# Edge values from the row's diagonal element, with a VectorE comparison of the whole matrix, in a two-layer graph kernel

## The chip, the cores and the metric

The kernel runs on one core of one Trainium2 chip. The metric is the device time of one execution in microseconds (us). Before the change the median of three runs is 389.42 us (389.2 to 390.23).

## The reference

2708 nodes have 128 features each, and a 2708 x 2708 matrix `adj` holds the weighted edges. In the inputs a row's nonzero elements are all equal (a 0/1 mask, with the diagonal always set, divided by the row's count). Layer 0 works on the hyperbolic ball:

```python
XW = mobius_matvec(W, X)
gamma = 2.0 / jnp.maximum(1.0 - jnp.sum(XW * XW, -1, keepdims=True), EPS)
nominator = A_hat @ (gamma * XW)
denominator = _clamp_abs(A_hat @ (gamma - 1.0))
...
x = _layernorm(x + _L0_gnn_ref(x, adj, L0_gnn_W), axis=-1)
```

Layer 1 passes a message over every edge, and the GELU stands inside the sum:

```python
s = x @ msg_w[:, :D].T
d = x @ msg_w[:, D:].T
messages = gelu(s[:, None, :] + d[None, :, :] + msg_b)
aggregated = einsum('ijd,ij->id', messages, adj)
h = gelu(concat([x, aggregated]) @ upd_w.T + upd_b) + x
x = _layernorm(x + layernorm(h) * ln_w + ln_b)
```

(Left out of layer 0: the Mobius scalings by 0.5 and by the row sum, log, relu and exp.) An edge that is zero contributes nothing, so only the nonzero elements of `adj` need a GELU. The kernel finds them on the chip.

## The kernel before

The 2708 rows are padded to 22 blocks of 128. The host sends `adj` transposed and tiled (`adj_t`, diagonal set to zero) and the diagonal apart, as columns of `pack` (`dg`).

**Layer 0**, `layer0(b)`, takes one block of rows. SyncE (SP) loads the transposed slab `aT` (128 x 2816 f32, 1408 KB, L317; two buffers). ScalarE (ACT) turns it into signs, `sgn`, and counts them (L319, 2.55 us, one buffer). TensorE (PE) multiplies the slab with the features `y`: 22 matmuls in fp32 (L324), which the generator interrupts at the tiles in `BREAKS` so that other work can be issued between them. VectorE (DVE) adds the diagonal's part (L328) and a few sums (L334).

**Edge lists.** `keys` multiplies the signs with bf16 keys, so that each target row holds numbers that encode the sources of its edges (L350), and DVE takes the largest eight of each segment (L358). `extract` turns them into lists of edges, in two stages. The first counts edges, makes prefix sums on PE (L397, L398) and builds `R`, a 128 x 128 matrix per list tile that says which row each of the 128 edges belongs to (L409 on ACT, L412 and L414 on DVE). The second multiplies `R` with the codes (L438), and gets for each edge its row number `rid` (L444) and its source `J` (L447). There are 25 lists in 99 list tiles of 128 edges. L448 then computes `F`, the flat position of the edge in `adj`, and for each of the 99 list tiles GpSimd (POOL) starts an indirect DMA that fetches 128 single elements into a column of `V` (L191, called from `extract`).

The order of the work is partly written out by hand: the loop at L543 to L569 steps the generators of three consecutive blocks alternately. The framework's scheduler then fixes each engine's queue, which runs in order.

`layer0_end` finishes blocks 0 to 15 as soon as they are there and blocks 16 to 21 at the end (`CHUNKS`). It is a long chain of small DVE operations with some ACT and PE, and it writes `d` of the reference to a table in HBM (L535, on SP's queue, which also issues the slabs). After it come the messages of nodes to themselves: `gd`, a GELU (L583) and one multiplication with the diagonal element per block (L585, 22 on ACT).

**Layer 1.** `messages` works through a block's list tiles, up to four at a time (a quad, 29 in all). POOL gathers the sources' rows of the table into `dd` (L191, 99 again, 512 bytes per edge). PE spreads `s` over the edges with `R` (L652). DVE adds (L657), ACT applies the GELU (L658). DVE builds `rv`, a matrix that has the edge's value at the edge's row (L654, one per list tile). PE multiplies `dd` with `rv` and accumulates a block in `ag` (L660). `own` adds the node's own message (L669). ACT copies `ag` out of PSUM (L691 and L702, 30 in all), and `update` and `finish` apply the last matmuls, GELU and normalizations. The buffers `dd` are a ring of seven quads (`RING`); the early tiles of blocks 2 to 7 are gathered into a slab buffer of layer 0. Tiles whose sources lie in blocks 0 to 15 (`soon`) may be gathered once the first half of the table is written. POOL's queue is in order too, so gathers into `V` and into `dd` stand in one line.

At the end a few counters are compared (`flags`, `cnt`), and a dense branch computes the result again if a list did not hold all edges. It isn't entered with these inputs.

The lines that matter:

```python
        F = small.tile([P, TMAX], U32, name="F", bufs=3)
...
            nc.vector.scalar_tensor_tensor(
                F[:, k0:k1], J[:, t], float(b * P * N - 1), rid[:, t], op0=OP.add, op1=OP.add
            )
        for t in range(t0, t0 + n):
            gather(V[:, t : t + 1], adj.rearrange("i (j o) -> (i j) o", o=1), F[:, t - t0 : t - t0 + 1])
...
                nc.vector.tensor_scalar(
                    rv[:, k, :], iotaN, rid[:, t : t + 1], V[:, t : t + 1], op0=OP.is_equal, op1=OP.mult
                )
```

Of the kernel before, what the change touches and what calls it, by code (L numbers as in the profile page):

```python
# [10 lines left out]
F32 = mybir.dt.float32  # L11
U32 = mybir.dt.uint32
# [3 lines left out]
OP = mybir.AluOpType  # L16
# [59 lines left out]
def hyperbolic_then_message_kernel(  # L76
# [4 lines left out]
    x_nm: bass.AP,  # L81
    x_t: bass.AP,
    pack: bass.AP,
    table: bass.AP,
    out: bass.AP,
):
# [79 lines left out]

    R = big.tile([P, NT, P], F32, name="R")
    J = const.tile([P, NT], U32, name="J")
    V = const.tile([P, NT], F32, name="V")
    rid = const.tile([P, NT], F32, name="rid")  # L170
    top = const.tile([P, NC], F32, name="top")
    limit = const.tile([P, NT], F32, name="limit")
# [5 lines left out]
    nc.gpsimd.memset(deg, 0.0)  # L178
    oe = const.tile([P, NL, 2], F32, name="oe")
    signs = const.tile([P, NB], F32, name="signs")  # L180
    poss = const.tile([P, NL], F32, name="poss")
    cap = const.tile([P, NL], F32, name="cap")
    least = const.tile([P, NL], F32, name="least")
# [6 lines left out]
    def gather(o, src, at):  # L190
        nc.gpsimd.indirect_dma_start(  # L191
            out=o, out_offset=None, in_=src, in_offset=bass.IndirectOffsetOnAxis(ap=at, axis=0)
        )
# [5 lines left out]
    def bank(name, bufs=2):  # L199
        return ps.tile([P, 512], F32, name=name, bufs=bufs)  # L200
# [10 lines left out]

    def cols(n):
        count[0] += 1
        return sc.tile([P, n], F32, name=f"c{count[0]}")

    def rsqrt(v, n, pool=None):

# [91 lines left out]
            y[:, g : g + n, :D], mx[:, g : g + n, :], c[:, g : g + n].unsqueeze(2).to_broadcast([P, n, D])  # L309
        )  # L310

    ss, ssp = cols(NB), cols(NB)

    def layer0(b):

        aT = stream.tile([P, NB, P], F32, name="aT")
        nc.sync.dma_start(aT, adj_t[b])  # L317
        sgn = stream.tile([P, NB, P], BF16, name="sgn", bufs=1)
        nc.scalar.activation(sgn, aT, AF.Sign, accum_out=signs[:, b : b + 1])  # L319
        op = bank("mp")  # L320
        for j in range(NB):
            if j in BREAKS:
                yield
            nc.tensor.matmul(  # L324
                op[:, : D + 2], lhsT=aT[:, j, :], rhs=y[:, j, :], start=(j == 0), stop=(j == NB - 1)
            )

        nc.vector.scalar_tensor_tensor(  # L328
            nom[:, b, :], y[:, b, :], dg[:, b : b + 1], op[:, : D + 2], op0=OP.mult, op1=OP.add
        )  # L330
        v, t = nom[:, b, :D], small.tile([P, D], F32, name="junk")
        nc.scalar.activation(t, v, AF.Square, accum_out=ss[:, b : b + 1])
        t = small.tile([P, D], F32, name="junk_p", bufs=1)
        nc.vector.scalar_tensor_tensor(  # L334
            t, v, 0.0, v, op0=OP.max, op1=OP.mult, accum_out=ssp[:, b : b + 1]
        )
        yield sgn
# [28 lines left out]
    def extract(l):  # L366
# [2 lines left out]
        C = wa + wb  # L369

        def tmp(name, dt=F32, w=CMAX):
            return small.tile([P, w], dt, name=name)[:, :C]

        tk = top[:, c0 : c0 + C]
        u0, u1 = 8 * (wa > 0), C - 8 * (wb > 0)
# [51 lines left out]
            )  # L427
        z = zs[l % 2][:, : C + 1]
        nc.vector.scalar_tensor_tensor(z[:, 1:], scan, SPAN, code, op0=OP.mult, op1=OP.add)
        F = small.tile([P, TMAX], U32, name="F", bufs=3)  # L430
        step = 512 // (C + 1)
        for k0 in range(0, n, step):
            k1 = min(n, k0 + step)
            w = k1 - k0
            t = slice(t0 + k0, t0 + k1)
            sp = bank("sel", 1)[:, : w * (C + 1)].rearrange("p (t c) -> p t c", t=w)
            for k in range(w):
                nc.tensor.matmul(sp[:, k, :], lhsT=R[:, t0 + k0 + k, :], rhs=z, start=True, stop=True)  # L438

            dist = small.tile([P, 512], F32, name="work", bufs=3)[:, : w * C].rearrange("p (t c) -> p t c", t=w)  # L440
            nc.vector.tensor_tensor(  # L441
                dist, sp[:, :, 1:], place[:, k0:k1].unsqueeze(2).to_broadcast([P, w, C]), op=OP.subtract
            )
            nc.scalar.copy(rid[:, t], sp[:, :, 0])  # L444
            near = small.tile([P, TMAX], F32, name="near")[:, :w]
            nc.vector.tensor_reduce(near, dist, axis=AX.X, op=OP.min, apply_absolute_value=True)
            nc.vector.scalar_tensor_tensor(J[:, t], near, -1.0, limit[:, t], op0=OP.add, op1=OP.min)  # L447
            nc.vector.scalar_tensor_tensor(  # L448
                F[:, k0:k1], J[:, t], float(b * P * N - 1), rid[:, t], op0=OP.add, op1=OP.add
            )  # L450
        for t in range(t0, t0 + n):
            gather(V[:, t : t + 1], adj.rearrange("i (j o) -> (i j) o", o=1), F[:, t - t0 : t - t0 + 1])

    x1, x1T = x_sb, xT
    s_nm = mx
# [1 line left out]
    def layer0_end(b0, b1):  # L457

        n = b1 - b0
        sb = slice(b0, b1)  # L460

        den, r = nom[:, sb, D], nom[:, sb, D + 1]
        di, t, v, e, f = (cols(n) for _ in range(5))
# [112 lines left out]

    gd = nom
    for ins in last.values():  # L580
        ctx.enter_context(tc.issue_after(ins.ins))
    for g, n in quads:
        nc.scalar.activation(gd[:, g : g + n, :D], gd[:, g : g + n, :D], AF.Gelu)  # L583
        for k in range(n):
            nc.scalar.mul(gd[:, g + k, :D], gd[:, g + k, :D], dg[:, g + k : g + k + 1])  # L585
    xlb = y
    for g, n in quads:
        nc.vector.tensor_add(xlb[:, g : g + n, :D], x1[:, g : g + n, :], wide(rowvec["lb"], n))
# [53 lines left out]
    def messages(b, ag, tiles, first, final, bins, room=ring):  # L642

        for q, k0 in enumerate(range(0, len(tiles), 4)):
            ts = tiles[k0 : k0 + 4]
            w = len(ts)
            dd = room(w)
            X = bank(bins[q % len(bins)]).rearrange("p (t d) -> p t d", d=D)[:, :w, :]
            rv = edge.tile([P, 4, P], F32, name="rv", bufs=3)
            for k, t in enumerate(ts):  # L650
                gather(dd[:, k, :], table[: SPLIT * P] if t in soon else table, J[:, t : t + 1])
                nc.tensor.matmul(X[:, k, :], lhsT=R[:, t, :], rhs=s_nm[:, b, :], start=True, stop=True)  # L652

                nc.vector.tensor_scalar(  # L654
                    rv[:, k, :], iotaN, rid[:, t : t + 1], V[:, t : t + 1], op0=OP.is_equal, op1=OP.mult
                )
            nc.vector.tensor_tensor(dd, X, dd, op=OP.add)  # L657
            nc.scalar.activation(dd, dd, AF.Gelu)  # L658
            for k in range(w):
                nc.tensor.matmul(  # L660
                    ag[:, :P],
                    lhsT=dd[:, k, :],
                    rhs=rv[:, k, :],
                    start=(first and k0 == 0 and k == 0),
                    stop=(final and k0 + k == len(tiles) - 1),
                )

    def own(b, ag):
        nc.tensor.matmul(ag[:, :P], lhsT=gd[:, b, :D], rhs=ident, start=True, stop=False)  # L669
# [17 lines left out]
    for b in range(EARLY):  # L687
        ag = bank("ag", 1)
        own(b, ag)
        messages(b, ag, early[b], False, True, ["X"], roomy)  # L690
        nc.scalar.copy(gd[:, b, :D], ag[:, :P])  # L691
    for g0, gn in GROUPS:
        h = gd[:, g0 : g0 + gn, :D]
        for b in range(g0, g0 + gn):
            ag = bank("mp")
            agT = edge.tile([P, P], F32, name="agT")
            if b < EARLY:
                messages(b, ag, late[b], True, True, ["X", "kx"])
            else:
                own(b, ag)  # L700
                messages(b, ag, early[b] + late[b], False, True, ["X", "kx"])
            nc.scalar.copy(agT, ag[:, :P])  # L702
            update(h, b - g0, b, [agT, gd[:, b, :D]] if b < EARLY else [agT])
        finish(h, g0, gn, fin, last=(g0 + gn == NB))

# [36 lines left out]
        flags[:, 1:2], flags[:, 1:2], float(P * sum(len(v[1]) for v in LISTS)), None, op0=OP.not_equal  # L742
    )

    cnt = sc.tile([P, 2], F32, name="cnt")
    nc.vector.tensor_reduce(cnt[:, 0:1], signs, axis=AX.X, op=OP.add)
    nc.vector.tensor_reduce(cnt[:, 1:2], deg.rearrange("p l k -> p (l k)"), axis=AX.X, op=OP.add)
    bp = bank("sel", 1)
    nc.tensor.matmul(bp[:, 0:2], lhsT=ones, rhs=flags, start=True, stop=True)
    nc.tensor.matmul(bp[:, 2:4], lhsT=ones, rhs=cnt, start=True, stop=True)  # L750
    tot = sc.tile([P, 4], F32, name="tot")
    nc.scalar.copy(tot, bp[:, 0:4])
    nc.vector.tensor_tensor(tot[:, 2:3], tot[:, 2:3], tot[:, 3:4], op=OP.not_equal)
    nc.vector.tensor_add(tot[:, 0:1], tot[:, 0:1], tot[:, 1:2])
    nc.vector.tensor_add(tot[:, 0:1], tot[:, 0:1], tot[:, 2:3])
    flag = sc.tile([P, 1], I32, name="flag")
    nc.vector.tensor_copy(flag, tot[:, 0:1])

    dense = nc.values_load(flag[0:1, 0:1], min_val=0, max_val=2 * P + 1)
    with tc.If(dense > 0):  # L760
        with tc.tile_pool(name="dn", bufs=1) as dn:
            room = R.rearrange("p t i -> p (t i)")
# [32 lines left out]
]  # L795


def by_partition(a, w):

    n = a.shape[0]  # L800
    nb = (n + P - 1) // P
    whole = np.zeros((nb * P, w), a.dtype)
    whole[:n] = a.reshape(n, w)
    return whole.reshape(nb, P, w).transpose(1, 0, 2).reshape(P, nb * w)


def layouts(x, adj, w0, msg_w, msg_b, upd_w, upd_b, ln_w, ln_b):
# [8 lines left out]
    xt[:, :n] = x.T  # L816
    parts = [w0] + [w[:, h * P : (h + 1) * P].T for w in (msg_w, upd_w) for h in (0, 1)]
    parts += [np.broadcast_to(v, (P, P)) for v in (upd_b, ln_w, ln_b, msg_b)]
    parts += [msg_b.reshape(P, 1), by_partition(np.diagonal(adj), 1)]
    return {  # L820
        "adj_t": np.ascontiguousarray(t),
        "x_nm": by_partition(x, P),
        "x_t": xt,
        "pack": np.ascontiguousarray(np.concatenate(parts, axis=1)),
    }


# [31 lines left out]
```

## Time and profile before

| | us |
|---|---|
| median of the runs | 389.42 |
| the profiled execution | 504.16 |
| its span, first to last instruction | 502.5 |
| PE busy | 333.5 |
| DVE busy | 275.9 |
| ACT busy | 208.0 |
| POOL busy | 203.5 |

A profile is one execution under the profiler. Here that execution is 114.7 us longer than the median run, so a length in the profile isn't a length in a run, while the duration of one instruction can be used. Busy time is the time in which an engine worked on an instruction; "mean ns" is the duration of one. A releaser is the instruction for which an engine waited. The stages in the profile: 0 to 26.5 us setup, to 293.7 us layer 0 (one L328 per block, at 38.2, 45.2, 57.0, 71.4, 85.2, 99.2, 119.8, 133.0, then every 7.7 to 8.7 us until 198.1, the last at 293.65), to 335 us the end of layer 0 for the last blocks, then layer 1. The last table gather starts at 451.75, the last matmul of `messages` ends near 473.

### The profile page before, as it was taken

Reading aid. Unit: us, or ns where it says so; the run is one execution under the profiler, and the core shown is the slowest. Engines: PE = TensorE matmul, PEld = TensorE weight load, DVE = VectorE, ACT = ScalarE, POOL = GpSimd, SP = SyncE. Lnnn points to the kernel's source line nnn. Section 1 sums busy time; section 2 is a strip of 40 time slices with the busy share of each in tenths; the row PEclk is TensorE's granted clock in tenths of the full one; section 3 lists DMA queues with packets and bytes.
Section 4 is the critical chain, followed back from the end, with each engine's and each line's share of the span. In section 5 each row is a group of like instructions: output and inputs, shape, how many; then the busy total and the mean of one; then the engine's idle time right before and its main releaser. Section 6 shows DMA issues by size and latency. Waiting matters only on the chain.

```text
span 502.5 us, 7784 instructions
## 1 busy us (share of the span) xinstructions
PE 333.5 (66%) x2427; PEld 297.2 (59%) x2427; DVE 275.9 (55%) x1474; ACT 208.0 (41%) x562; POOL 203.5 (40%) x297
## 2 busy tenths in 40 slices
PE   4269788674899989797973111538397697679620
PEld 4269677564889878795862001338395576557410
DVE  2979546433666565798740067248272226376671
ACT  2827325432657465794650022135032112326521
POOL 5301454571644525222257707722616572470000
PEclk9759779885999999998995555657679557798855
DMA  8306322223345544433421101110201120111100
GB/s 341 167 2 232 115 84 79 88 98 116 118 132 214 193 156 164 184 117 115 137 80 37 52 7 31 52 53 15 49 12 37 42 54 17 38 42 48 32 23 20
DMA packets 16237, 45.14 MB, mean 90 GB/s; under 512 B 5626, under 2 KB 11150, under 8 KB 13374
## 3 DMA queue, kind: packets, MB, share of 16 engines
q1 hardware_dynamic: 9710, 37.43, 20.6%
q0 software_dynamic: 6336, 6.55, 5.4%
q10 hardware_dynamic: 144, 0.60, 0.4%
q8 instruction: 20, 0.33, 0.3%
q14 instruction: 27, 0.22, 0.1%
HBM read 41.74 MB, written 2.83 MB: 89 GB/s over the span
## 4 chain that ended last, share of the span: by engine, by line
PE 32%; DVE 21%; issue 16%; another core or an unknown queue 14%; ACT 10%; DMA 4%; POOL 1%; DVEq 0%; POOLq 0%; ACTq 0%; SPq 0%
PE mp L324 7%; PE X L652 4%; PE mp L660 4%; PE kx L350 4%; PE sel L438 3%; DVE top L358 2%; ACT nom L635 2%; ACT sgn L319 2%; PE ag L660 2%; PE sel L612 1%; PE sel L613 1%; PE sel L610 1%; DMA xT<-in_x_t_dram 1%; DMA V<-in_adj_dram,F 1%
## 5 line engine op out<-in xcount | busy, mean ns | idle before, releaser
L191 POOL DMA_INDIRECT V<-in_adj_dram,F x99 | 94.9, 959 | 156.2 <-DVE top L358 31.0
L324 PE MATMUL mp<-y,aT 128*128 128x130 f32 x968 | 129.2, 288 | 1.4 <-DVE y L308 0.9
L324 PEld LDWEIGHTS mp<-y,aT 128*128 128x128 f32 x968 | 120.1, 199 | 2.3 <-DVE y L308 1.1
L191 POOL DMA_INDIRECT dd<-table_dram,J x81 | 78.1, 965 | 83.7 <-ACT agT L702 21.7
L319 ACT ACTIVATE sgn<-aT 128x2816 bf16<-128x2816 f32 x22 | 56.1, 2548 | 24.5 <-issue 20.5
L350 PE MATMUL kx<-kd,sgn 128*128 128x128 bf16 x484 | 41.5, 240 | 26.6 <-issue 19.1
L350 PEld LDWEIGHTS <-sgn 128*128 128x128 bf16 x484 | 33.3, 108 | 40.1 <-issue 31.4
L652 PE MATMUL X<-mx,R 128*128 128x128 f32 x198 | 41.1, 357 | 16.9 <-DVE dd L657 6.9
L654 DVE TENSOR_SCALAR rv<-iotaN,rid,V 128x128 f32<-128x128 f32 x99 | 30.1, 351 | 32.6 <-remote 20.0
L652 PEld LDWEIGHTS X<-mx,R 128*128 128x128 f32 x198 | 36.2, 265 | 19.2 <-DVE dd L657 7.5
L438 PE MATMUL sel<-z,R 128*128 128x49 f32 (+4 forms) x198 | 31.4, 299 | 23.3 <-DVE R L414 9.6
L438 PEld LDWEIGHTS sel<-z,R 128*128 128x128 f32 x198 | 28.3, 213 | 25.8 <-DVE R L414 10.4
L358 DVE MAX8 top<-kx 128x8 f32<-128x128 f32 (+3 forms) x152 | 28.6, 236 | 19.9 <-remote 14.8
L441 DVE TENSOR_TENSOR work<-sel,place 128x144 f32<-128x144 f32 (+11 forms) x29 | 11.7, 403 | 40.5 <-remote 30.9
L409 ACT ACTIVATE work<-iota,mid 128x512 f32<-128x512 f32 (+3 forms) x53 | 26.8, 553 | 5.5 <-DVE mid L402 5.4
L657 DVE TENSOR_TENSOR dd<-X,dd 128x384 f32<-128x384 f32 (+3 forms) x29 | 15.2, 526 | 21.7 <-remote 7.5
L444 ACT COPY rid<-sel 128x3 f32<-128x3 f32 (+5 forms) x29 | 4.7, 162 | 46.0 <-DVE work L441 36.3
L660 PE MATMUL mp<-rv,dd 128*128 128x128 f32 x116 | 21.6, 321 | 3.1 <-ACT dd L658 3.1
L402 DVE SCALAR_TENSOR_TENSOR mid<-sel,deg 128x2 f32<-128x2 f32 x25 | 3.9, 155 | 35.7 <-ACT oe L399 35.7
L610 PE MATMUL sel<-pk,xT 128*128 128x128 f32 x44 | 12.6, 377 | 16.4 <-ACT nom L614 10.4
L658 ACT ACTIVATE dd<-dd 128x384 f32<-128x384 f32 (+3 forms) x29 | 13.7, 497 | 20.3 <-DVE dd L657 14.5
L399 ACT COPY oe<-sel 128x2 f32<-128x2 f32 x25 | 4.0, 159 | 43.2 <-PE kx L350 25.9
(204 smaller groups left out, 614.6 us busy)
## 6 DMA issues: line engine op xcount, KB each, us to landing
aT<-in_adj_t_dram SPq DMA_DIRECT2D x22, 1408.0 KB, 6.7
V<-in_adj_dram,F POOLq DMA_INDIRECT x99
xT<-in_x_t_dram SPq DMA_DIRECT2D x2, 704.0 KB
x_sb<-in_x_nm_dram SPq DMA_DIRECT2D x2, 704.0 KB
out_dram<-nom SPq DMA_DIRECT2D x21, 64.0 KB, 1.6
dd<-table_dram,J POOLq DMA_INDIRECT x81
table_dram<-dt SPq DMA_DIRECT2D x5, 256.0 KB
pk<-in_pack_dram ACTq DMA_DIRECT2D x1, 587.5 KB
```

The lines of the kernel that those rows point to most:

```text
L191: nc.gpsimd.indirect_dma_start(out=o, out_offset=None, in_=src, in_offset=bass.IndirectOffsetOnAxis(ap=at, axis=0))
L319: nc.scalar.activation(sgn, aT, AF.Sign, accum_out=signs[:, b : b + 1])
L324: nc.tensor.matmul(op[:, : D + 2], lhsT=aT[:, j, :], rhs=y[:, j, :], start=(j == 0), stop=(j == NB - 1))
L350: nc.tensor.matmul(kp[:, i * P : (i + 1) * P], lhsT=sgn[:, j, :], rhs=kd[:, q, :], start=False, stop=(i == len(groups) - 1 and j == j1 - 1),)
L358: nc.vector.max(top[:, c : c + 8], seg[:, s, :])
L409: nc.scalar.activation(r0, iota[:, k0 * P : k1 * P], AF.Abs, scale=2.0, bias=mid[:, k : k + 1])
L438: nc.tensor.matmul(sp[:, k, :], lhsT=R[:, t0 + k0 + k, :], rhs=z, start=True, stop=True)
L610: nc.tensor.matmul(up[:, :D], lhsT=x1T[:, s], rhs=wT[:, 2, :], start=True, stop=False)
L652: nc.tensor.matmul(X[:, k, :], lhsT=R[:, t, :], rhs=s_nm[:, b, :], start=True, stop=True)
L654: nc.vector.tensor_scalar(rv[:, k, :], iotaN, rid[:, t : t + 1], V[:, t : t + 1], op0=OP.is_equal, op1=OP.mult)
L657: nc.vector.tensor_tensor(dd, X, dd, op=OP.add)
L660: nc.tensor.matmul(ag[:, :P], lhsT=dd[:, k, :], rhs=rv[:, k, :], start=(first and k0 == 0 and k == 0), stop=(final and k0 + k == len(tiles ...
```

## The change

All of a row's edges take the row's diagonal element as their value. That makes the values unnecessary inside the sum: `rv` becomes 0/1, the own message is no longer multiplied, and the sum `ag` is multiplied with the diagonal once per block (`scaled`), while it is copied out of PSUM. A new input `diag` holds the diagonal as one row; it is loaded broadcast over the partitions, once per block in layer 0 (`vb`, on SP's queue) and once per copy in layer 1 (`v`, on ACT's queue). The gathers of `V` and the positions `F` go. In layer 0, DVE compares every element of the slab with the diagonal element of its row and counts the equal ones; at the end the count must be the number of edges, and the diagonal must be positive, or the dense branch is taken. Some small buffers become single, and the columns of `cols` are reused between the stages.

```diff
@@ def cols
-        return sc.tile([P, n], F32, name=f"c{count[0]}")
+        return sc.tile([P, NB], F32, name=f"c{count[0]}")[:, :n]
...
@@ def layer0
+        vb = stream.tile([P, P], F32, name="vb")
+        nc.sync.dma_start(vb, diag[:, b * P : (b + 1) * P].to_broadcast([P, P]))
         aT = stream.tile([P, NB, P], F32, name="aT")
         nc.sync.dma_start(aT, adj_t[b])
         sgn = stream.tile([P, NB, P], BF16, name="sgn", bufs=1)
         nc.scalar.activation(sgn, aT, AF.Sign, accum_out=signs[:, b : b + 1])
+
+        eq = stream.tile([P, NB, P], mybir.dt.uint8, name="eq", bufs=1)
+        nc.vector.scalar_tensor_tensor(
+            eq, aT, 1.0, vb.unsqueeze(1).to_broadcast([P, NB, P]),
+            op0=OP.mult, op1=OP.is_equal, accum_out=same[:, b : b + 1],
+        )
...
@@ def extract
-            return small.tile([P, w], dt, name=name)[:, :C]
+            return small.tile([P, w], dt, name=name, bufs=2 if name in ("m", "whole") else 1)[:, :C]
...
-        F = small.tile([P, TMAX], U32, name="F", bufs=3)
...
-            nc.vector.scalar_tensor_tensor(
-                F[:, k0:k1], J[:, t], float(b * P * N - 1), rid[:, t], op0=OP.add, op1=OP.add
-            )
-        for t in range(t0, t0 + n):
-            gather(V[:, t : t + 1], adj.rearrange("i (j o) -> (i j) o", o=1), F[:, t - t0 : t - t0 + 1])
...
@@ own messages
         nc.scalar.activation(gd[:, g : g + n, :D], gd[:, g : g + n, :D], AF.Gelu)
-        for k in range(n):
-            nc.scalar.mul(gd[:, g + k, :D], gd[:, g + k, :D], dg[:, g + k : g + k + 1])
...
@@ def messages
-                nc.vector.tensor_scalar(
-                    rv[:, k, :], iotaN, rid[:, t : t + 1], V[:, t : t + 1], op0=OP.is_equal, op1=OP.mult
+            k = 0
+            while k < w:
+                n = next((i for i in range(1, w - k) if ts[k + i] != ts[k] + i), w - k)
+                nc.vector.tensor_tensor(
+                    rv[:, k : k + n, :],
+                    iotaN.unsqueeze(1).to_broadcast([P, n, P]),
+                    rid[:, ts[k] : ts[k] + n].unsqueeze(2).to_broadcast([P, n, P]),
+                    op=OP.is_equal,
                 )
+                k += n
...
+    def scaled(o, b, ag):
+
+        v = edge.tile([P, P], F32, name="v")
+        nc.scalar.dma_start(v, diag[:, b * P : (b + 1) * P].to_broadcast([P, P]))
+        nc.vector.tensor_mul(o, ag[:, :P], v)
...
-        nc.scalar.copy(gd[:, b, :D], ag[:, :P])
+        scaled(gd[:, b, :D], b, ag)
...
-            nc.scalar.copy(agT, ag[:, :P])
+            scaled(agT, b, ag)
...
+    nc.vector.tensor_reduce(cnt[:, 2:3], same, axis=AX.X, op=OP.add)
+
+    low = sc.tile([P, 1], F32, name="lowest")
+    nc.vector.tensor_reduce(low, dg, axis=AX.X, op=OP.min)
+    nc.vector.scalar_tensor_tensor(flags[:, 1:2], low, 0.0, flags[:, 1:2], op0=OP.is_le, op1=OP.add)
...
```

## The prediction

> **What bounds the kernel now.** I read the busy shares first, then a table of the stages, then the chain of waits by stage, then POOL's and ACT's timelines where layer 1 begins.
>
> The table of stages has, for each stretch, its length, then the busy time of PE, weight loads, DVE, ACT and POOL, the granted clock and the DMA share. The stretches are blocks 0 to 7, 8 to 15, 16 to 20, block 21, the end of layer 0, the middle of layer 1, the tail:
>
> ```profile
> PE 333.5 (66%) x2427; PEld 297.2 (59%) x2427; DVE 275.9 (55%) x1474; ACT 208.0 (41%) x562; POOL 203.5 (40%) x297
> ...
> 26.50:133.00 106.50, 80.56 (x631) 74.11 (x631) 60.21 (x331) 43.92 (x115) 43.24 (x45) 0.81 0.28 96
> 133.00:198.10 65.10, 61.32 (x608) 57.56 (x605) 41.40 (x238) 41.01 (x97) 28.90 (x31) 1.00 0.51 179
> 198.10:253.30 55.20, 49.24 (x418) 44.15 (x417) 45.32 (x275) 37.76 (x92) 14.29 (x15) 0.97 0.43 150
> 253.30:293.70 40.40, 14.21 (x104) 10.86 (x104) 5.93 (x36) 6.39 (x18) 25.48 (x27) 0.64 0.13 36
> 293.70:335.00 41.30, 11.36 (x36) 8.40 (x35) 21.06 (x141) 8.84 (x27) 22.24 (x23) 0.54 0.14 39
> 335.00:472.00 137.00, 102.30 (x563) 89.67 (x564) 72.40 (x306) 45.19 (x133) 56.44 (x58) 0.75 0.13 33
> 472.00:502.50 30.50, 5.50 (x20) 4.10 (x20) 13.82 (x93) 9.88 (x28) 1.43 (x2) 0.51 0.11 31
> ```
>
> No engine is full over the span, but stages differ. In blocks 8 to 15 PE is busy 94%, and DVE 64%. In blocks 16 to 20 DVE is at 82%, because the end of layer 0 for blocks 0 to 15 falls there.
>
> The chain of waits, whole page first, then for 258 to 300 us alone:
>
> ```profile
> PE 32%; DVE 21%; issue 16%; another core or an unknown queue 14%; ACT 10%; DMA 4%; POOL 1%; DVEq 0%; POOLq 0%; ACTq 0%; SPq 0%
> ...
> by line: issue 59.0%; PE kx L350 11.8%; PE mp L324 8.8%; PE sel L438 3.0%; DVE top L358 1.9%; DVE R L412 1.5%; DVE R L414 1.3%; PE kx L344 1.3%; ACT work L409 1.2%; DVE scan L424 0.8%; DVE mid L402 0.8%; DVE c L227 0.5%; DVE c L229 0.5%; DV
> ```
>
> These are pauses that no dependence explains. One crawl of PE on L350, from 268.6 to 292, takes 23 us for 22 matmuls that take 1.4 us in other blocks. "Unknown queue" is 14.3% of 502.5, 72 us; "issue" is 25 us of 258 to 300 and 13 us of 300 to 340. Together 110 us, nearly the 114.7 us by which the profiled execution (504.16) exceeds the median (389.42). The pauses lie beside unbroken runs of gathers on POOL. I conclude that the timed runs lack them, and take a run as the profile without them: blocks 0 to 7 net of the chain's 30 us, 76; blocks 8 to 15, 65; 16 to 20, about 54 (196 in all); block 21, 12; end of layer 0, 28. Layer 1 starts near 262 then.
>
> POOL where the table becomes ready, and ACT before the first message:
>
> ```profile
> L191 POOL DMA_INDIRECT V<-in_adj_dram,F x99 | 94.9, 959 | 156.2 <-DVE top L358 31.0 <-DVE F L448 30.2 <-DVE mid L402 29.5
> ...
> 255.02 0.94 POOL L191 DMA_INDIRECT dd<-table_dram,J  x1 [11.36 <-DMA table_dram<-dt]
> 256.26 0.94 POOL L191 DMA_INDIRECT V<-in_adj_dram,F  x1 [0.30 <-issue]
> 257.51 0.94 POOL L191 DMA_INDIRECT V<-in_adj_dram,F  x1 [0.31 <-issue]
> ...
> 342.09 1.85 ACT L585 ACTIVATE nom<-nom,pk 128x128 f32<-128x128 f32 x6
> 343.84 2.38 ACT L658 ACTIVATE dd<-dd 128x512 f32<-128x512 f32 x5
> ...
> 451.75 0.94 POOL L191 DMA_INDIRECT dd<-table_dram,J  x1 [1.60 <-ACT agT L702]
> 471.89 1.16 PE L660 MATMUL mp<-rv,dd 128*128 128x128 f32 x6 [2.33 <-ACT dd L658]
> ```
>
> A gather holds POOL for 0.95 us and 0.30 us more. Until 255 POOL has half its time free: V gathers there cost nothing. After it nine V gathers share the queue with the 99 of `dd`. But the last `dd` gather starts at 451.75 and PE ends the messages 20 us later: there the consumers set the pace, and POOL waits for their buffers.
>
> **What the Trainium skill says.** "VectorE: DVE Perf Modes", section "The TRN2 errata", gives (N+151)/0.96 ns for an fp32 add of two tensors, and "The perf-mode tier table" says that such an operation stays at one element per cycle. The trace agrees: 128x512 took 0.69 us, 128x256 0.42. "DMA: Bandwidth & Descriptors", section "SWDGE vs HWDGE vs iDMA", says that GpSimd computes the descriptors of its own DMAs in software, which fits the 0.95 us. "Perfetto Trace Analysis", section "Summary: the profiler window per engine type", says that matmul ends are estimated; here DVE's L358 starts 2.2 us after the recorded end of L350, so I count DVE time and stage lengths rather than PE's ends.
>
> **The change, part by part.**
>
> 1. The comparison `eq`, 22 times 128x2816 on DVE. Two-tensor rows give 1.04 ns per element and 0.156 fixed (0.42 and 0.69 us), so 3.09 us, and the accumulator read 0.083 as at L389: 3.17 us, 69.8 us in all. Below, 1.6 us, if the byte output let it run at two per cycle, which no row suggests; above, 3.5 for the broadcast operand. I take 3.17.
>
> 2. `F` goes: 29 times 0.16, 4.7 us of DVE.
>
> 3. Where 1 and 2 land. Up to block 20 DVE has 60.2 + 41.4 + 45.3 = 147 us of work in 196 us. It becomes 147 + 69.8 - 4.7 = 212. DVE can't do that in 196 us: it becomes the bound of layer 0, at least +16. It won't be full all the time, since its queue is in order and waits for PE and ACT; it was 99% full in the second block (7.00 of 7.05 us) and 98% in 216.5 to 227.9. At 96% the stage takes 221 us, +25. By stage: blocks 0 to 7 from 76 to about 86, 8 to 15 from 65 to 70, 16 to 20 from 54 to 64. Setup hides none of it: DVE is occupied by a chain of small operations from 9.6 us on, and the first slab is due only after the two other loads. At 90% it is +40; if two comparisons do find room in setup, +18. I take +25.
>
> 4. `vb`, 22 broadcasts of 64 KB on SP's queue, 0.33 us of issue each as for L317: hidden beside the slabs (6.7 us to landing, 8 us per block). But SP now waits for the comparison of two blocks before as well, since it frees `aT` and `vb`, and the table writes L535 stand behind it. That is in the +25, as both follow DVE.
>
> 5. V gathers go: 99 times 1.25, 124 us of POOL. The first 90 are hidden. The nine after 255 are worth 11.2 us if POOL sets the pace of layer 1, nothing if the consumers do. The 20 us lag says consumers; I take -2.
>
> 6. L585 goes: 22 multiplications, 6.7 us of ACT in 335.5 to 343.9. The first L658 follows the last of them at 343.84, while its input was ready at 340.5: -3.3, after which DVE's L588 and L657 are late.
>
> 7. `rv` in quads: 99 times 0.35 (30.1 us busy) become 29 of the shapes of L657 (15.2 us): -15 of DVE in layer 1. DVE is 72 of about 105 net us there, mostly off the path; waits of PE for L657 total 6.9. I take -3 (0 to -8).
>
> 8. `scaled`: 30 times a DVE product of 0.29 to 0.34 us (L657 128x128, L328 with PSUM) for ACT's 0.26, and it queues behind DVE's sums and statistics, with PE's L612 waiting for it. I take +0.1 each, +3 (0 to +12). The 30 broadcasts `v` cost ACT 0.33 each, 10 us beside the 45 it has, and land in about 1.6 us (as the 64 KB output does), hidden if the scheduler issues them a block ahead; two buffers allow that. If not, up to 1.6 each.
>
> 9. Single buffers, reused columns, three more operations for flags (0.2 us each): nothing. The small buffers are written and read by DVE in order, and the flags were done at 480.6, beside `finish`. Without that cover, 1.
>
> Sum: +25 - 2 - 3.3 - 3 + 3 = +20 against the profiled execution's counted work. I carry it unchanged to the median: 389.4 + 20 = 409. The profiled execution itself should shrink, not grow, since most pauses beside V gathers go with them (30 us before 133, up to 25 at block 21).
>
> **Rivals.** *Badly packed comparisons* (the scheduler puts them before the extraction that PE waits for): DVE 90% full, +40 - 5 = 424. For it: each block has a round trip DVE, PE, ACT, DVE. Against it: DVE's 99% in the second block.
> *Consumers follow POOL*: without pauses PE is faster and POOL may run unbroken, 108 gathers of 1.25 from the table on; then item 5 is -11, item 7 -8, and with two comparisons hidden +18 the sum is about 0: 389. Against it the 20 us lag.
> *The pauses are partly real* (the faster side): bursts of V gathers hold PE's instruction stream in timed runs too. Place: layer 0, 30 us before 133 and 25 at block 21. Price: what share is real; at two thirds, -37, which gives 389 + 20 - 37 = 372. It decides from 20 of the 55 us, a share of 36%. For it: they lie exactly beside the bursts. Against it: with them the run can't be 389.
>
> **How the numbers follow.** The forecast, 409, has a chance of 0.52 (own range 398 to 418); badly packed 0.22; POOL's pace 0.08; real pauses 0.18. A difference of 0.3% is about what a measurement of this kernel can tell from no change. POOL's pace gives half its chance to no change and a quarter to each side. Faster 0.20, same 0.04, slower 0.76. The range reaches from 386 to 426: it leaves out most of the real pauses and the worst packing.
>
> **What would show it.** Right: `eq` near 3.17 us each, DVE above 90% in blocks 0 to 20, the wait for DVE behind ACT's L319 and PE, layer 1 somewhat shorter net of pauses. Item 6 shows in the first L658 right behind L583; item 8 in PE's L612 waiting for DVE; item 5 in `dd` gathers unbroken after the table. Wrong: `eq` at half the time, or a timed gain as large as the profiled one.

## The result, and the profile after

The changed kernel takes 435.86 us (median of 4 runs, 433.91 to 438.33), the kernel before 389.83 in the same comparison: a ratio of 1.1183, with an interval of 1.1121 to 1.1245. The loss is 46 us, where the prediction said 20. Ratios in this document compare only executions in the faster of two states, so on some chips they differ a little from the quotient of the medians. The profiled execution took 433.91 us (span 432.2) and is one of the timed runs, so nothing has to be taken out of it.

The page of the kernel after: busy shares, the chain of waits by engine and by line, and the groups that say most (busy time and mean ns, then the idle time ahead of them with its releaser).

```profile
PE 309.5 (72%) x2427; PEld 279.5 (65%) x2427; DVE 323.0 (75%) x1459; ACT 198.4 (46%) x510; POOL 112.7 (26%) x198
...
PE 33%; DVE 28%; DMA 22%; ACT 6%; issue 5%; POOL 3%; SPq 0%; POOLq 0%; ACTq 0%; DVEq 0%
PE mp L333 16%; DMA aT<-in_adj_t_dram 13%; DVE eq L325 6%; PE sel L446 4%; DMA dd<-table_dram,J 4%; POOL dd L192 3%; PE kx L359 2%; PE X L655 2%; DMA v<-in_diag_dram 2%; DMA table_dram<-dt 2%; ACT nom L638 2%; PE ag L670 2%; DVE top L367 2%
...
L192 POOL DMA_INDIRECT dd<-table_dram,J x81 | 82.3, 1016 | 267.3 <-DVE work L449 242.9
...
L325 DVE SCALAR_TENSOR_TENSOR eq<-aT,vb 128x2816 uint8<-128x2816 f32 x22 | 67.7, 3079 | 0.0
L322 ACT ACTIVATE sgn<-aT 128x2816 bf16<-128x2816 f32 x22 | 56.1, 2549 | 24.4 <-DMA aT<-in_adj_t_dram 21.2
```

Two things are new. The comparison takes 3.08 us each, with no idle time of DVE ahead of it. And the load of the slab `aT`, which the chain hardly met before, is now 13% of it: ACT's sign pass idles 21.2 us for slabs. The item "another core or an unknown queue", 14% before, is gone.

The stages of the kernel after (length; busy time of PE, weight loads, DVE, ACT, POOL; clock, DMA share): blocks 0 to 7, 8 to 15, 16 to 20, from there to the first gather of table rows, the gathers, the tail.

```profile
26.50:115.80 89.30, 76.95 (x662) 71.13 (x661) 76.03 (x329) 48.22 (x115) 0.00 (x0) 0.88 0.35 119
115.80:183.70 67.90, 61.53 (x597) 58.02 (x596) 57.92 (x245) 39.73 (x95) 0.00 (x0) 0.97 0.52 179
183.70:231.00 47.30, 32.91 (x293) 31.47 (x291) 41.58 (x214) 26.47 (x69) 0.00 (x0) 0.91 0.38 130
231.00:259.70 28.70, 20.80 (x132) 16.08 (x132) 19.97 (x94) 14.07 (x31) 0.00 (x0) 0.80 0.28 88
259.70:389.40 129.70, 94.34 (x627) 83.85 (x626) 87.44 (x386) 42.50 (x111) 99.80 (x99) 0.82 0.29 71
389.40:432.20 42.80, 14.16 (x70) 10.93 (x69) 23.77 (x148) 13.86 (x38) 1.46 (x3) 0.62 0.11 30
```

DVE is the busiest engine only in part of layer 0, and nowhere is it above 90%: 85%, 85% and 88% in the first three rows. PE is at 86% and 91% in the first two. No engine is full, yet the stages are longer. What they wait for shows in the timeline of two blocks (start, duration, engine, operation, and in brackets the idle time before):

```profile
138.16 3.07 DVE L325 SCALAR_TENSOR_TENSOR eq<-aT,vb 128x2816 uint8<-128x2816 f32 x1
...
141.27 0.33 SPq L318 DMA_DIRECT2D vb<-in_diag_dram  x1
141.70 0.37 SPq L320 DMA_DIRECT2D aT<-in_adj_t_dram  x1
...
146.11 3.07 DVE L325 SCALAR_TENSOR_TENSOR eq<-aT,vb 128x2816 uint8<-128x2816 f32 x1
...
149.46 3.18 PE L333 MATMUL mp<-y,aT 128*128 128x130 f32 x26 [1.09 <-DMA aT<-in_adj_t_dram]
149.52 2.55 ACT L322 ACTIVATE sgn<-aT 128x2816 bf16<-128x2816 f32 x1 [1.81 <-DMA aT<-in_adj_t_dram]
```

A comparison ends at 141.2; SP at once issues the next `vb`, and then the next slab. It is there at 149.46, when PE has been idle for it for 1.1 us and ACT for 1.8. This slab's own comparison starts at 154.96, 5.5 us after it landed, and ends at 158.04; only then may the slab after the next be loaded into the same buffer. So the comparison is the last reader of its slab, and its place in DVE's queue sets when loads begin. In the waits of SP's queue this shows too: 68.8 us in 8 waits directly for comparisons, while without a comparison the slab loads wait for PE (169.1 us in 19 waits).

### The profile page after: what moved, and what is told of

Its sections match the earlier page's. It is cut to its first block, busy times and chain, and to the rows that moved or that the text cites. A ratio compares the mean times of both kernels' runs of the same rounds, so it can differ in the third digit from the quotient of the medians.

```text
span 432.2 us, 7651 instructions
## 1 busy us (share of the span) xinstructions
PE 309.5 (72%) x2427; PEld 279.5 (65%) x2427; DVE 323.0 (75%) x1459; ACT 198.4 (46%) x510; POOL 112.7 (26%) x198
## 4 chain that ended last, share of the span: by engine, by line
PE 33%; DVE 28%; DMA 22%; ACT 6%; issue 5%; POOL 3%; SPq 0%; POOLq 0%; ACTq 0%; DVEq 0%
PE mp L333 16%; DMA aT<-in_adj_t_dram 13%; DVE eq L325 6%; PE sel L446 4%; DMA dd<-table_dram,J 4%; POOL dd L192 3%; PE kx L359 2%; PE X L655 2%; DMA v<-in_diag_dram 2%; DMA table_dram<-dt 2%; ACT nom L638 2%; PE ag L670 2%; DVE top L367 2%; PE X L532 1%; DMA xT<-in_x_t_dram 1%
## 5 line engine op out<-in xcount | busy, mean ns | idle before, releaser
L192 POOL DMA_INDIRECT dd<-table_dram,J x81 | 82.3, 1016 | 267.3 <-DVE work L449 242.9
L325 DVE SCALAR_TENSOR_TENSOR eq<-aT,vb 128x2816 uint8<-128x2816 f32 x22 | 67.7, 3079 | 0.0
L322 ACT ACTIVATE sgn<-aT 128x2816 bf16<-128x2816 f32 x22 | 56.1, 2549 | 24.4 <-DMA aT<-in_adj_t_dram 21.2
L359 PE MATMUL kx<-kd,sgn 128*128 128x128 bf16 x484 | 34.6, 225 | 10.3 <-ACT sgn L322 10.3
L655 PE MATMUL X<-mx,R 128*128 128x128 f32 x198 | 31.4, 292 | 13.3 <-DVE dd L667 11.8
L446 PE MATMUL sel<-z,R 128*128 128x49 f32 (+4 forms) x198 | 29.7, 288 | 13.1 <-DVE R L423 9.1
L655 PEld LDWEIGHTS X<-mx,R 128*128 128x128 f32 x198 | 26.8, 201 | 15.6 <-DVE dd L667 13.3
L446 PEld LDWEIGHTS sel<-z,R 128*128 128x128 f32 x198 | 26.7, 203 | 14.9 <-DVE R L423 9.8
L367 DVE MAX8 top<-kx 128x8 f32<-128x128 f32 (+3 forms) x152 | 32.7, 237 | 0.7 <-PE kx L359 0.6
L449 DVE TENSOR_TENSOR work<-sel,place 128x144 f32<-128x144 f32 (+11 forms) x29 | 11.7, 405 | 27.1 <-PE sel L446 27.0
L668 ACT ACTIVATE dd<-dd 128x384 f32<-128x384 f32 (+3 forms) x29 | 14.0, 498 | 36.2 <-DVE dd L667 26.5
L660 DVE TENSOR_TENSOR rv<-iotaN,rid 128x384 f32<-128x384 f32 (+3 forms) x35 | 18.3, 528 | 3.4 <-PE mp L670 2.3
L192 POOL DMA_INDIRECT aT<-table_dram,J x18 | 17.6, 976 | 5.5 <-issue 4.9
L670 PEld LDWEIGHTS mp<-rv,dd 128*128 128x128 f32 x116 | 17.6, 226 | 2.0 <-ACT dd L668 1.2
L617 ACT ACTIVATE nom<-sel 128x128 f32<-128x128 f32 x22 | 6.0, 272 | 25.8 <-PE sel L616 23.6
```

What stands on the lines that cost most here:

```text
L192: nc.gpsimd.indirect_dma_start(out=o, out_offset=None, in_=src, in_offset=bass.IndirectOffsetOnAxis(ap=at, axis=0))
L325: nc.vector.scalar_tensor_tensor(eq, aT, 1.0, vb.unsqueeze(1).to_broadcast([P, NB, P]), op0=OP.mult, op1=OP.is_equal, accum_out=same[:, b ...
L359: nc.tensor.matmul(kp[:, i * P : (i + 1) * P], lhsT=sgn[:, j, :], rhs=kd[:, q, :], start=False, stop=(i == len(groups) - 1 and j == j1 - 1),)
L367: nc.vector.max(top[:, c : c + 8], seg[:, s, :])
L660: nc.vector.tensor_tensor(rv[:, k : k + n, :], iotaN.unsqueeze(1).to_broadcast([P, n, P]), rid[:, ts[k] : ts[k] + n].unsqueeze(2).to_broad ...
L670: nc.tensor.matmul(ag[:, :P], lhsT=dd[:, k, :], rhs=rv[:, k, :], start=(first and k0 == 0 and k == 0), stop=(final and k0 + k == len(tiles ...
```

## Experiments

Each engine's order of instructions is laid out anew for each kernel, so a few microseconds between two of them are not a mechanism. The clearest measure is the moment at which the table is ready (POOL's first gather of table rows). From 17 us, where the first blocks begin, to there is layer 0. The kernel before has no profile of an execution of 389 us, so the kernel without a comparison stands in for it:

| kernel | table ready, us | from 17 us | DVE busy in it | share | table to end of span | time |
|---|---|---|---|---|---|---|
| no comparison | 213.0 | 196.0 | 153.7 | 78% | 172.1 | 386.87 |
| 1 tile of 22 | 223.8 | 206.8 | 156.7 | 76% | 171.5 | 396.7 |
| 11 tiles | 224.9 | 207.9 | 177.6 | 85% | | |
| 16 tiles | 232.2 | 215.2 | 189.7 | 88% | 174.7 | 407.52 |
| 22, of a resident tile | 237.6 | 220.6 | 203.1 | 92% | 173.9 | 414.78 |
| the same, after the signs | 242.1 | 225.1 | 203.7 | 91% | | |
| 22, at high priority | 252.5 | 235.5 | 206.3 | 88% | 175.3 | 428.3 |
| the change | 259.7 | 242.7 | 204.6 | 84% | 172.5 | 435.86 |

Empty cells are kernels that ran only on chips with pauses, of which more below. The last two columns already settle one point: layer 1 takes 171.5 to 175.3 us whenever it starts. A delay of the table passes to the end in full, and the whole loss arises ahead of the table.

Two cautions. The comparisons ahead of the table last 66 us in the change, but DVE's busy time there grows by 51 (153.7 to 204.6): in a fuller queue the records of neighbouring instructions overlap more. And PE is busy 12 us longer in the change's layer 0 than without a comparison (193.2 and 181.6), at a granted clock of 0.89 instead of 0.94; with the resident tile it is 192.6 at 0.90, so the clock does not tell these kernels apart.

**No comparison.**

```diff
-        vb = stream.tile([P, P], F32, name="vb")
-        nc.sync.dma_start(vb, diag[:, b * P : (b + 1) * P].to_broadcast([P, P]))
...
-        nc.vector.scalar_tensor_tensor(
-            eq, aT, 1.0, vb.unsqueeze(1).to_broadcast([P, NB, P]),
-            op0=OP.mult, op1=OP.is_equal, accum_out=same[:, b : b + 1],
-        )
...
-    nc.vector.tensor_reduce(cnt[:, 2:3], same, axis=AX.X, op=OP.add)
+    nc.vector.tensor_reduce(cnt[:, 2:3], signs, axis=AX.X, op=OP.add)
```

> The changed kernel without the comparison and without the row vb; the count of equal elements is left out (the count of signs stands in for it), all else stays. If the comparison is the whole cause of the loss, the table is ready near 220 us instead of 259.7 and the time is 385 to 393 us, no slower than before (389.8). If layer 1 lost too (the rows v, the products that replace copies, rv in quads), it stays above 397 us. If the removed gathers of values had been worth more than the 2 us that the prediction gave them, it is below 380 us.

Measured: 386.87 us beside 389.47, ratio 0.9925 (0.9897 to 0.9953). The comparison, with the row that it needs, is the whole cause of the loss; all the rest of the change together is a gain of 2.6 us. Its stages, for blocks 8 to 15 and then for all of layer 0:

```profile
97.60:158.40 60.80, 60.80 (x615) 57.84 (x613) 41.19 (x233) 41.68 (x100) 0.00 (x0) 1.00 0.54 191
...
17.00:213.04 196.04, 181.56 (x1683) 169.13 (x1684) 153.68 (x877) 130.85 (x335) 0.00 (x0) 0.94 0.43 155
```

In blocks 8 to 15 PE is busy all 60.80 us, 7.6 a block, and DVE 41.19, 5.15 a block. The room on DVE is thus 2.45 us a block; the comparison needs 3.16.

**Held slab or VectorE's time.** Two kernels were meant to take these apart. One compares a single tile: almost no time, but the comparison still reads the slab. The other compares all 22 tiles of `xT`, which is resident: full time, and no slab is held (the row `vb` is still loaded).

```diff
-            eq, aT, 1.0, vb.unsqueeze(1).to_broadcast([P, NB, P]),
+            eq[:, :1, :], aT[:, NB - 1 :, :], 1.0, vb.unsqueeze(1).to_broadcast([P, 1, P]),
```

> The comparison reads one tile of the slab instead of 22 (the other 21 are left out of the count): the slab is still held until VectorE has come to it, and vb is still loaded, but the time on VectorE is a few tenths of a us instead of 3.1. If VectorE's time is the cause, the time is within 5 us of the kernel without a comparison. If the cause is that the comparison holds the slab and the next load starts late, it is 15 us or more above the kernel without one, near 410 to 430 us.

```diff
-            eq, aT, 1.0, vb.unsqueeze(1).to_broadcast([P, NB, P]),
+            eq, xT.rearrange("p (b d) -> p b d", d=P), 1.0, vb.unsqueeze(1).to_broadcast([P, NB, P]),
```

> The comparison has its full size but reads xT, which is resident, instead of the slab (so the count of equal elements is left out): 3.1 us of VectorE each, and no slab is held. If VectorE's time is the cause, the time is 420 to 436 us. If the held slab is the cause, it is 385 to 405 us.

Measured: 396.7 us (ratio 1.0196, 1.011 to 1.0283) and 414.78 (1.065, 1.0595 to 1.0706). Neither expectation holds alone: one tile costs 10 us with hardly any work, and the work costs 28 without holding a slab. The waits (total us, times, longest) in the change:

```profile
ACT sgn L322 <- DMA aT<-in_adj_t_dram: 21.2, 12, 2.9
PEld mp L333 <- DMA aT<-in_adj_t_dram: 20.6, 14, 4.2
PE mp L333 <- DMA aT<-in_adj_t_dram: 14.7, 13, 2.7
```

With one tile they are smaller at PE, and the comparison itself waits at the head of DVE's queue:

```profile
DVE eq L325 <- DMA aT<-in_adj_t_dram: 21.6, 11, 3.4
PEld mp L333 <- DMA aT<-in_adj_t_dram: 4.1, 5, 1.1
```

So the one-tile kernel does not measure a held slab. Its comparison comes as soon as the slab has landed and is over 0.3 us later, long before PE is done with the slab. What it holds is the small row `vb`, and SP's queue, which runs in order, has the next row standing ahead of a slab:

```profile
139.00 0.29 DVE L325 SCALAR_TENSOR_TENSOR eq<-aT,vb 128x128 uint8<-128x128 f32 x1 [3.41 <-DMA aT<-in_adj_t_dram]
139.33 0.33 SPq L318 DMA_DIRECT2D vb<-in_diag_dram  x1
139.76 0.38 SPq L320 DMA_DIRECT2D aT<-in_adj_t_dram  x1
```

Counted from the start, these are the comparison of block 13, the row of block 15 and the slab of block 14. PE had left that slab's buffer at 136.45, but the load stood behind a row that waited for the comparison, and the comparison had waited for the slab before. In the change each row of blocks 4 to 20 stands directly ahead of its own slab, so it does not lose time in this way.

With the resident tile no engine waits for a slab load at all in the list of waits, and DVE has nearly the same work as in the change, 203 us, packed at 92% into layer 0:

```profile
17.00:237.58 220.58, 192.56 (x1753) 177.95 (x1754) 203.07 (x918) 132.44 (x333) 0.00 (x0) 0.90 0.43 148
```

A second form of it takes the slab's sum of signs as its scalar, so that each comparison comes when its slab is there, still without holding it. It is put in at high priority, and no row is loaded.

```diff
-        nc.sync.dma_start(vb, diag[:, b * P : (b + 1) * P].to_broadcast([P, P]))
...
+        with tc.high_priority():
...
-            eq, aT, 1.0, vb.unsqueeze(1).to_broadcast([P, NB, P]),
+                eq, xT.rearrange("p (b d) -> p b d", d=P), signs[:, b : b + 1], y[:, 0, :D].unsqueeze(1).to_broadcast([P, NB, P]),
```

> The full-size comparison reads xT (so the count of equal elements is left out) and waits for the slab's sum of signs, but holds no slab; vb is not loaded. Some 18 of the 22 comparisons then stand before the table is ready. If held slab (9.8 us by the one-tile run) and VectorE's time add up to the 49 us, this one is 386.9 plus 18/22 of 39, so 414 to 424 us. If VectorE's time hurts only through the held slab, it is below 400.

Its chip was one with pauses (488.48 us beside 503.82), so its time answers nothing. Its table was ready at 242.1, with 21 comparisons ahead of it. VectorE's time alone is therefore worth 24.5 to 29 us of layer 0 (220.6 and 225.1 against 196.0). The 18 to 22 us that are left to 242.7 come with the comparison's reading the slab. They are idle time of DVE: 38 us in the change's layer 0, 17.5 and 21 in these two. Most of it stands behind PE: the step L449, which needs PE's selection L446, waits 24.9 us there, against 7.3 and 9.0 us.

**The comparison earlier in the queue.**

```diff
+        with tc.high_priority():
+            eq = stream.tile([P, NB, P], mybir.dt.uint8, name="eq", bufs=1)
+            nc.vector.scalar_tensor_tensor(
...
```

> The changed kernel with the comparison at high priority, so that most of the comparisons stand directly behind the sum nom of the block before instead of some ten instructions ahead of their own block's. If the held slab is the cause, loads start earlier and the time falls by 8 to 25 us, to 411 to 428. If VectorE's time is the cause, it stays within 5 us of 435.9, or grows where VectorE waits for a slab at the head of its queue.

Measured: 428.3 us (1.0978, 1.0908 to 1.1048), 7.6 less than the change; the wait for slabs at PE and ACT is gone from the list. The direction speaks for the held slab, but the size lies just under the lower edge. With no wait of PE or ACT for slabs left, layer 0 still takes 235.5 us, 10 to 15 more than with VectorE's time alone. PE now waits more for DVE's extraction (18 us for `R` and `z`, 9.5 in the change), which fits comparisons that stand ahead of the extraction of other blocks. So late loads are not shown to make up all of the 18 to 22 us; the order of comparisons and extraction in DVE's queue, which each kernel has of its own, may be part of them, and no run takes the two apart.

**How the loss grows with size.** The edit for 16 tiles; for 11 it has `NB // 2` in their place:

```diff
-            eq, aT, 1.0, vb.unsqueeze(1).to_broadcast([P, NB, P]),
+            eq[:, :16, :], aT[:, NB - 16 :, :], 1.0, vb.unsqueeze(1).to_broadcast([P, 16, P]),
```

> The comparison reads 11 tiles of 22 (the others are left out of the count): 1.6 us instead of 3.1. If each microsecond on VectorE costs alike, the time lies halfway between the one-tile run and the full one, 413 to 420 us. If VectorE has room for the first 30 us and is the bound only from there on, it is 398 to 409. If the first half costs most, 424 or more.

> The comparison reads 16 tiles of 22 (the other 6 are left out of the count), 2.25 us each. Read by the moment at which the table is ready, which is the same on all chips (223.8 us with one tile, 224.9 with 11, 259.7 with 22): if VectorE has room for about the first 30 us and is the bound from there on, 238 to 244 us. If the room ends later and the rest costs more than its own length, 226 to 236. If the step lies between 11 and 16 tiles, 246 or more.

With 11 tiles the table is ready at 224.1 to 224.9 us (three chips): 12 us later than without a comparison, for 22 comparisons of 1.7 us, 37 in all. (Its times, 478.24, 472.95 and 473.01 us, are from chips with pauses; on one without, no time was taken.) That it comes only 1 us after the one-tile kernel says little, as that one pays for its row. With 16 tiles the table is ready at 232.2 and the time is 407.52 (1.0429, 1.0361 to 1.0498). That misses my first value: the last six tiles, 18 us of VectorE, cost 27.5 us. The waits change there: with 11 and 16 tiles SP's slab loads still wait mostly for PE (110.1 and 101.2 us), and PE's waits for slabs come to 1.3 us at most. With 22 the comparison has become the slab's last reader.

The room of 2.45 us a block, which 16 tiles keep (2.3 us) and 22 exceed, is only part of this. The sum `nom` of block 15 comes at 158.4 us without a comparison, at 158.2 with 16 tiles and at 183.7 with 22, but with the resident tile, at full length, at 153.5. VectorE's time is not free there; it is put off. Of the 25 lists 18 have been begun by then without a comparison, 14 with 16 tiles and 11 with the resident tile, and from there to the table it takes 54.6, 74.0 and 84.1 us.

**Half of it in layer 1.** All of the comparison: 11 tiles in layer 0, and 11 that are loaded again into a free slab buffer in layer 1.

```diff
+    def rest_of(b):
...
+        part = spare[:, (b % 2) * n : (b % 2 + 1) * n, :]
+        nc.sync.dma_start(part, adj_t[b][:, HALF:, :])
...
+        nc.vector.scalar_tensor_tensor(
+            eq[:, :n, :], part, 1.0, vb.unsqueeze(1).to_broadcast([P, n, P]),
+            op0=OP.mult, op1=OP.is_equal, accum_out=same[:, NB + b : NB + b + 1],
+        )
```

> All of the comparison, half in each layer. Where before takes 389 us: 396 to 406 us if layer 1, paced by GpSimd, has room for 34 us more on VectorE; 410 to 425 if the comparisons stall VectorE's queue there or the loads delay the gathers. Where before takes 491 to 504: 478 to 493 again.

Measured: 422.99 us (1.0876, 1.0796 to 1.0956): 13 less than the change, and still far slower than before. My value was wrong. The table was ready at 224.8, but layer 1 took 194.8 us instead of 172. The gathers and the tail of the split kernel, then of the kernel without a comparison:

```profile
224.80:368.83 144.03, 102.56 (x613) 90.46 (x613) 106.18 (x389) 41.81 (x109) 109.66 (x98) 0.77 0.52 155
368.83:419.60 50.77, 16.78 (x82) 13.20 (x80) 34.01 (x188) 14.11 (x39) 2.37 (x3) 0.60 0.33 94
```

```profile
213.04:340.50 127.46, 94.43 (x634) 83.66 (x630) 85.57 (x385) 42.91 (x110) 97.35 (x99) 0.83 0.31 72
340.50:385.10 44.60, 17.51 (x68) 14.18 (x68) 23.55 (x146) 13.65 (x37) 1.43 (x2) 0.52 0.11 29
```

The first row of the split kernel ends where its last gather starts. To the end of the last gather it took 145.0 us, in the other kernel 127.2, so the gathers took 17.8 us longer and what follows 5. Of the 17.8 us some 13 are gathers that last longer, mostly beside comparisons, and 4.5 are one stop of GpSimd that the profile does not explain. DVE and POOL of the split kernel:

```profile
283.05 1.62 DVE L702 SCALAR_TENSOR_TENSOR eq<-aT,vb 128x1408 uint8<-128x1408 f32 x1 [0.19 <-DVE rv L661]
```

```profile
281.90 0.94 POOL L193 DMA_INDIRECT dd<-table_dram,J  x1 [0.30 <-issue]
283.15 2.33 POOL L193 DMA_INDIRECT dd<-table_dram,J  x1 [0.30 <-PE ag L671]
```

The gather that starts at 283.15, during the comparison, takes 2.33 us instead of 0.94 and ends 0.8 us after it. Over layer 1, 29 of the 99 gathers exceed 1.05 us, by 17.1 us beyond 0.94 in all; without a comparison it is 13, by 4.0. Of the 29, 20 overlap a comparison, with 14 of the 17 us, and 17 of these end 0.8 us after it. That VectorE had 63 us to spare there was true, but its work is not free for GpSimd. Whether the second loads, which raise the DMA share of the gathers' stage from 0.31 to 0.52, cost time as well was not tested.

**Whose pauses?** The prediction took 110 us of pauses out of the profile of before, as something that timed runs lack.

```diff
+    nc.gpsimd.memset(V, 1.0)
...
-        for t in range(t0, t0 + n):
-            gather(V[:, t : t + 1], adj.rearrange("i (j o) -> (i j) o", o=1), F[:, t - t0 : t - t0 + 1])
```

> The kernel before without the gathers of values and without their indices F (V is set to 1, so the values of the edges are left out). If the pauses beside the gathers are in the profile alone, the profiled execution shrinks from 504 to within 1% of the timed median. If the gathers cost nothing when timed, the median is 385 to 390 us; if GpSimd paces layer 1, so that the nine gathers of values behind the table count, it is 376 to 383; if the pauses are partly real in the timed runs, it is below 375.

> The kernel before, for its profile. On a chip where it takes 389 us, its profiled execution takes 389 too if the pauses belong to the chip: table ready near 215 us, layer 1 near 172 us. If they belong to the profiler, about 504 again.

> The changed kernel as it is. On a chip where the kernel before takes 389 us it takes 433 to 438 again. On a chip with pauses beside the gathers (before 501 us or more) its table is ready near 260 us, and layer 1 takes the 247 to 254 us that it took in the other kernels there: 505 to 516 us, 0 to 3% slower than before instead of 12%, because the gathers of values, which cost the kernel before some 40 us of pauses ahead of the table, are gone.

On three chips the kernel before took 497 to 504 us (medians), and its profiled execution as long; on the others its runs took 389 to 391 (medians). The pauses are thus real there, and not the profiler's. Each chip was used at one time only, and the three directly one after another, so whether they belong to the chip or to a condition of that time stays open, and so does their cause. They stand beside gathers of either kind. Without the gathers of values the kernel before took 469.35 us beside 503.82 (0.9459, 0.9348 to 0.957; once more, 0.9351), its table was ready at 212.3, as without pauses, and the pauses began with the gathers of rows. Its page and one stage of it:

```profile
PE 50%; another core or an unknown queue 17%; DVE 16%; ACT 7%; issue 6%; DMA 2%; POOLq 0%; ACTq 0%; DVEq 0%; POOL 0%
...
233.00:290.00 57.00, 2.71 (x10) 2.04 (x9) 17.44 (x129) 6.37 (x21) 23.07 (x25) 0.50 0.11 29
```

In 57 us PE was busy 2.71. With the gathers of values the table came at 253.2 on such a chip (501.03 us), so they cost 41 us of layer 0 there. The change removes these and adds its 47: on such a chip it takes 506.4 us, 1.026 of before (1.0162 to 1.0359), instead of 1.118. The change with the gathers put back beside the comparison:

> The changed kernel with the gathers of values put back beside the comparison; what they fetch is not used. Timed, 434 to 440 us if the gathers of values cost nothing, 445 to 452 if those behind the table delay the gathers of rows. The profiled execution is longer than the timed one again, by 60 us or more, if the pauses belong to the gathers of values.

It took 525.46 us (512.9 to 527.46) beside 503.82, with the table at 284.1: a chip with pauses again, so the two values of the expectation were not told apart. The split kernel, 486.95 and 488.57 us there (0.9647 and 0.9717), is faster than before on those chips. No version was found that beats the kernel before where it takes 389 us; there the whole room is the 2.6 us of the kernel without a comparison.

## Why the prediction was wrong

The direction was right, for a reason that the prediction gave only in part; the size was too small by more than a factor of two. By its steps:

- *Step 1*, 3.17 us for a comparison: 3.08 and 0.083 for the accumulator. Right.
- *Steps 2 and 3*, DVE becomes the bound and costs +25: as VectorE's time alone it measured 24.5 to 29. That agreement is luck, as three errors cancel. Counted from 26.5 us to the table, as the step counts, layer 0 without a comparison takes 186.5 us, not 196; DVE's busy time with the full comparisons is 194 to 196 us, not 212; and the fill is 91 to 92% where no slab is held, not 96%. With the true 186.5 the step's own 221 us would have given +34.
- *Step 4* failed: "But SP now waits for the comparison of two blocks before as well [...] That is in the +25, as both follow DVE." It is not in the +25. Layer 0 grew by 46.7 us, and 18 to 22 of them come with the comparison's reading the slab. The wait had been seen, and was priced at nothing without a sum. In the timeline above the loop reads: 5.5 us from a slab's landing to its comparison, 3.1 for that, 0.5 until the next load is issued, 7.8 for the load. That is 16.9 us, over two buffers 8.4 a block. Blocks 8 to 15 took 8.5 each, where they take 7.6 without a comparison and with the resident tile as well. PE and ACT are late by it, and DVE idles in turn, so a fill of 92% became 84%. For the other blocks the share of the late loads, against that of the order in DVE's queue, stays open.
- By stage: blocks 0 to 7 rose by 18 us (put at 10), 8 to 15 by 7 (5), from there to the table by 21 (10), each against the kernel without a comparison.
- *Steps 5 to 8*, together -5.3: measured -2.6 (-4.0 to -1.8) for all of the change but the comparison. Step 5 chose wrongly between its two cases: after the table POOL runs without a break, 99 gathers in 129.7 us. What the nine gathers less were worth was not measured apart. Step 6: the first message comes at 305.58, after 2.67 us of waiting for DVE, and not right behind the pass over `gd`. Step 7: `rv` takes 18.3 us, 15 were put. Step 8: `v` lands in 3.0 us, not 1.6; the waits of DVE for it sum to 3.7 us.
- *The net reading of the profile of before* held in that runs of 389 us leave no room for such pauses. Its layer 0 was 9.5 us too long, as said. Its reason fell: the pauses are not in the profile alone.
- *Rivals.* The badly packed comparisons gave 424 and came nearest, with DVE 90% full; it was 84%. Where PE and ACT no longer wait for slabs, 10 to 15 us beyond VectorE's time remain, so packing is not excluded as part of the cause beside the slabs. POOL's pace came true, but not the sum of 389 that it was to give. Real pauses exist, but not in the runs of the result; and where they exist they make up for the loss nearly, not more.

## What to carry to other kernels

Price a second reader of a streamed buffer twice. Once as time, against what its engine has to spare; here 16 of 22 tiles fitted into the blocks and still cost 19 us of layer 0, since other work was put off. And once as a loop: from the landing of a slab through the reader's place in its queue to the landing of the next slab in the same buffer (here 8.4 us a block, where PE needs 7.6). An operation of full length on resident data measures the first. A tiny one on the streamed buffer measures the second only if its trace shows the same path; here it took another, through a small row ahead of the slabs in SP's queue. And before taking something out of a profile that disagrees with the timed runs, see whether it is in other executions of the same program elsewhere.

## What had not been expected of the hardware

This comparison, a VectorE operation with two inputs in SBUF, holds up a GpSimd gather that starts beside it. In the change, for the last slab, first DVE and then POOL:

```profile
260.51 3.08 DVE L325 SCALAR_TENSOR_TENSOR eq<-aT,vb 128x2816 uint8<-128x2816 f32 x1
```

```profile
261.24 3.16 POOL L192 DMA_INDIRECT dd<-table_dram,J  x1 [0.31 <-issue]
264.71 0.95 POOL L192 DMA_INDIRECT dd<-table_dram,J  x1 [0.30 <-issue]
```

3.16 us instead of 0.95, ending 0.8 us after the comparison. The Trainium skill names a reason in "SBUF — State Buffer", section "SBUF: two separate sides": VectorE and GpSimd share a port pair under an exclusive lock, which a VectorE operation takes with two SBUF inputs against a GpSimd operation that reads SBUF. The trace agrees with that, as the gather takes its indices from SBUF; no run here tests the lock against another cause. The change itself hardly pays for it, as 21 of its comparisons come before the first gather, but it is most of what makes layer 1 a poor place for the other half.

Second, executions of one program differ by far more than noise: the same kernel before took 389 to 391 us on some chips and 497 to 504 on three, with pauses of PE, DVE and ACT beside GpSimd's gathers, and the ratio of the change went from 1.118 to 1.026.
